# A mixture-of-experts loop re-staged: five turns a page, results queued behind sends, routing in single parts, and a second mixture in four pieces

## The chip, the cores and the metric

One core of one Trainium2 chip runs the whole program. The metric is the device time of one execution in microseconds (us). The engines are TensorE (PE in the profile; PEld is its weight load), VectorE (DVE), ScalarE (ACT), GpSimd (POOL) and SyncE (SP, which only issues DMAs). Each engine works through its own queue in order.

## What is computed

A residual network in float32 on x of shape (4, 1024, 256), four layers one after the other:

```python
x = x + retention(layernorm(x))     # 16 heads, decay mask, gated, group-normalised
x = x + moe(layernorm(x))           # 8 experts, 2 for each token
x = x + rwkv6(layernorm(x))         # a recurrent scan over 1024 steps, 16 heads
x = x + moe(layernorm(x))           # the same router and experts again
```

The mixture is what the change is about:

```python
def moe(t):                                     # t: 4096 tokens x 256
    probs = softmax(t @ Wg.T + bg)              # 8 experts
    topw, topi = top_k(probs, 2)
    topw = topw / sum(topw)
    for e in range(8):                          # combine[:, e] is the token's share, or 0
        gate, up = split(t @ w1[e].T)           # 256 -> 2 x 256
        out += combine[:, e] * ((silu(gate) * up) @ w2[e].T)
    return out
```

## The kernel before

The 4096 tokens are 32 tiles of 128 rows, and eight blocks of four tiles (`NBLK`, `NT`); the residual of block `bk` stays in the on-chip memory as `res[bk]`.

**Pages.** Each mixture computes each token for its two experts only. Tokens are sorted into pages of 128 rows; a page belongs to one expert. 2 x 32 + 7 = 71 pages (`NSL`) always suffice. A token tile is normalised, tagged with its two shares and its number, and written twice into the page buffer `xg_all` in HBM by an indirect DMA that GpSimd issues (`send`, L788). The page loop loads pages in groups of four (`get`, L821), computes, and scatters each page's 128 result rows by another indirect DMA of GpSimd to `y_all` in HBM (`down`, L879). Later `ask` (L916) loads a token tile's two results back and `take` (L927) adds them to the residual on VectorE.

**Pieces.** Tokens come in pieces (`Piece`). The first holds blocks 0 to 3; then follow two pieces of two blocks, here called mid and end. The first piece alone is sure to fill 25 pages (`FULL`); a load of those pages waits for the first piece's sends only, and every load from page 25 on waits for all sends. A piece is routed when its logits are there: `logits` (L549) normalises four tiles on ScalarE, transposes them on TensorE, multiplies with the router, transposes back; `routing` (L597) is a generator whose six parts, called one by one through `route`, pick the two experts (parts one and two, VectorE), rank tokens within an expert by two small matmuls (part three), and work out each token's row (parts four to six). `table` (L759) finds which expert each page belongs to.

**The page loop** (`tiles`, L897) is software-pipelined over three turns. The code of turn j, in the order in which every engine gets it:

```python
if j + 1 < NSL: self.fetch(j + 1)    # transpose page j+1 (PE), copy to m_xt (ACT)
if j < NSL:     self.up(j)           # m_hp (PE), silu m_sg (ACT), product m_a (DVE)
...
if 0 <= j - 1 < NSL: self.turn(j - 1)   # transpose m_a (PE), copy to m_aT (DVE)
if j > 1:            self.down(j - 2)   # m_op (PE), scale to m_y (ACT), scatter (POOL)
for f, *a in extra.get(j, ()): f(*a)    # other work planned for this turn
```

In both mixtures the queues of TensorE, ScalarE, VectorE and GpSimd hold exactly this written order (`manual_schedule`). `extra` holds the rest: routing and sends of the later pieces, `ask` and `take` of the first 16 tiles from turn 41 on, in the first mixture also the end of the retention (`rest`) and the preparation of the scan's first block (`prepare`, L1344), in the second the end of the scan (`finish`, L1383).

**Around it.** The retention runs 32 chunks (loop at L1519); the first piece of the first mixture is sent from chunk 26 on, and the second piece's logits are made in chunks 29 and 31. Then w2a is loaded (L1556) and the page loop starts. During the scan the second mixture's first piece is routed and sent. After the second page loop the last 16 tiles are asked for and taken (L1688 to L1691), and each finished block is stored (`done`, L944).

## Time and profile before

| | |
|---|---|
| Timed runs | 1568.88 us (median of 3, 1567.33 to 1575.58) |
| Profiled execution | 1572.42 us, of which 1570.6 us is the span from first to last instruction |
| Mean granted TensorE clock | 0.918 |
| First page loop, first to last m_sg | 357.7 to 649.1 us |
| Second page loop, first to last m_sg | 1278.4 to 1540.1 us |
| Last scatter issued | 1545.3 us |

The costliest groups in the two page loops, from the page. Columns: line, engine, operation, output <- inputs, count; then busy us in all and mean ns of one; then the idle time of that engine just before such instructions and what ended most of it.

```profile
L888 POOL DMA_INDIRECT y_all<-m_y,m_to x142 | 137.7, 969 | 299.8 <-ACT m_xt L840 169.7
L845 PE MATMUL m_hp<-w1a,m_xt 128*128 x568 | 287.1, 630 | 14.3 <-ACT m_xt L840 11.0
L882 PE MATMUL m_op<-w2a,m_aT 128*128 x568 | 150.8, 389 | 12.0 <-DVE m_aT L877 7.1
L794 POOL DMA_INDIRECT xg_all<-m_row,m_at x128 | 125.1, 977 | 48.7 <-issue 32.6
L838 PE MATMUL m_xtp<-cst,m_xg 128*128 128x128 f32 x284 | 57.9, 288 | 6.1 <-DMA m_xg<-xg_all 6.1
```

A matmul's mean is longer than its share of the time, because matmuls overlap; 142 is two mixtures of 71 pages. A line of slices in the page has 40 digits, one for each fortieth of the span (39.3 us), in tenths.

### The profile page before, as it was taken

How to read it: one execution, taken by the hardware profiler on the slowest of the kernel's cores; microseconds unless marked ns; L12 is line 12 of the kernel's file. 1: busy time of each engine (PE TensorE's matmuls, PEld its weight loads, DVE VectorE, ACT ScalarE, POOL GpSimd, SP SyncE). 2: the span in 40 equal slices, each digit the busy share in tenths (PEclk: the TensorE clock that was granted, in tenths of full speed). 3: DMA queues.
4: the chain of work that ended last, by engine and by line, in shares of the span. 5: the costliest groups of instructions: out<-in, count | busy, mean ns of one | idle time of the engine just before them, and what ended most of it. 6: DMA issues, size and time to landing. Idle time of an engine off the chain costs nothing.

```text
span 1570.6 us, 21231 instructions
## 1 busy us (share of the span) xinstructions
PE 1323.9 (84%) x6700; PEld 680.1 (43%) x6700; DVE 997.4 (64%) x1914; ACT 645.7 (41%) x1646; POOL 892.1 (57%) x854
## 2 busy tenths in 40 slices
PE   5999998958889989998979797889787567899993
PEld 3666665635446544422223232233222124456561
DVE  6666667425433343299978788989998963433544
ACT  2343434333533333445535464545445143433331
POOL 4233323643553225399988888887789935543331
PEclk9999999978789999998979798989898688999997
DMA  8992111131332341267665454534555831332645
GB/s 294 327 320 78 55 55 54 63 118 54 131 112 90 120 125 62 64 144 181 161 143 150 119 135 120 141 101 121 134 161 136 243 112 65 113 99 85 195 125 184
DMA packets 117549, 207.72 MB, mean 132 GB/s; under 512 B 12192, under 2 KB 80000, under 8 KB 117440
## 3 DMA queue, kind: packets, MB, share of 16 engines
q1 hardware_dynamic: 95904, 160.20, 36.3%
q0 software_dynamic: 17184, 39.86, 8.2%
q10 hardware_dynamic: 4352, 6.29, 1.3%
q8 instruction: 57, 0.93, 0.3%
q14 instruction: 52, 0.43, 0.1%
HBM read 139.18 MB, written 67.14 MB: 131 GB/s over the span
## 4 chain that ended last, share of the span: by engine, by line
PE 51%; DVE 16%; POOL 15%; ACT 7%; issue 6%; DMA 3%; another core or an unknown queue 1%; SPq 0%; POOLq 0%; DVEq 0%; ACTq 0%
PE m_hp L845 14%; POOL w_s L1177 7%; PE m_op L882 6%; DVE w_s L1169 4%; PE w_pp L1081 4%; PE a_qkp L311 3%; POOL w_xf L1047 2%; PE a_yp L370 2%; DVE w_vb L1167 2%; POOL w_xf L1050 2%; PE m_xtp L838 2%; PE a_gp L293 2%; PE m_atp L875 2%; PE a_op L245 2%; PE a_sp L350 2%
## 5 line engine op out<-in xcount | busy, mean ns | idle before, releaser
L1177 POOL TENSOR_TENSOR w_s<-w_s,w_rT 128x1024 f32<-128x1024 f32 x128 | 304.5, 2415 | 39.3 <-DVE w_s L1169 29.5
L888 POOL DMA_INDIRECT y_all<-m_y,m_to x142 | 137.7, 969 | 299.8 <-ACT m_xt L840 169.7
L845 PE MATMUL m_hp<-w1a,m_xt 128*128 x568 | 287.1, 630 | 14.3 <-ACT m_xt L840 11.0
L851 DVE TENSOR_TENSOR m_a<-m_hp,m_sg 128x256 f32<-128x256 f32 x142 | 60.1, 423 | 274.4 <-ACT m_sg L849 257.7
L1169 DVE TENSOR_TENSOR_SCAN w_s<-w_wk,w_carry,w_vb 128x512 f32<-128x512 f32 x128 | 160.9, 1276 | 17.0 <-ACT w_carry L1187 4.6
L1167 DVE TENSOR_TENSOR w_vb<-w_vb,w_wk 128x1024 f32<-128x1024 f32 x128 | 153.1, 1196 | 17.1 <-ACT w_wk L1110 15.9
L1169 DVE TENSOR_TENSOR_SCAN w_s<-w_wk,w_vb 128x512 f32<-128x512 f32 x128 | 152.8, 1215 | 14.6 <-PE w_yp L1200 7.4
L882 PE MATMUL m_op<-w2a,m_aT 128*128 x568 | 150.8, 389 | 12.0 <-DVE m_aT L877 7.1
L794 POOL DMA_INDIRECT xg_all<-m_row,m_at x128 | 125.1, 977 | 48.7 <-issue 32.6
L845 PEld LDWEIGHTS m_hp<-w1a,m_xt 128*128 128x128 f32 x568 | 103.8, 203 | 91.4 <-issue 77.6
L1200 PE MATMUL w_yp<-w_s,core_c 128*32 128x512 f32 x512 | 97.0, 672 | 41.7 <-POOL w_s L1177 33.2
L849 ACT ACTIVATE m_sg<-m_hp 128x256 f32<-128x256 f32 x142 | 54.4, 383 | 167.8 <-PE m_hp L845 143.3
L887 ACT ACTIVATE m_y<-m_op,m_share 128x256 f32<-128x256 f32 x142 | 67.2, 473 | 119.1 <-PE m_op L882 90.0
L882 PEld LDWEIGHTS m_op<-w2a,m_aT 128*128 128x128 f32 x568 | 98.8, 194 | 23.8 <-ACT m_y L887 9.4
L323 POOL TENSOR_TENSOR a_t<-a_t,a_t 128x512 f32<-128x512 f32 x32 | 41.0, 1282 | 117.5 <-DVE a_t L322 95.1
L1047 POOL TENSOR_TENSOR w_xf<-w_xf,w_sx 128x512 f32<-128x512 f32 x60 | 78.2, 1303 | 33.2 <-ACT w_xf L1046 32.6
L353 DVE TENSOR_TENSOR a_pt<-a_sp,ret_c 128x2048 f32<-128x2048 f32 x32 | 73.2, 2286 | 17.1 <-PE a_sp L350 17.0
L875 PEld LDWEIGHTS m_atp<-cst,m_a 128*128 128x128 f32 x284 | 40.4, 145 | 89.5 <-issue 70.8
L1050 POOL TENSOR_TENSOR w_xf<-w_xf,w_xT 128x512 f32<-128x512 f32 x64 | 69.7, 1090 | 6.1 <-DVE w_xf L1044 1.4
L840 ACT COPY m_xt<-m_xtp 128x256 f32<-128x256 f32 x142 | 51.9, 365 | 29.4 <-PE m_xtp L838 28.2
L875 PE MATMUL m_atp<-cst,m_a 128*128 128x128 f32 x284 | 55.7, 278 | 9.0 <-DVE m_a L851 5.7
L838 PE MATMUL m_xtp<-cst,m_xg 128*128 128x128 f32 x284 | 57.9, 288 | 6.1 <-DMA m_xg<-xg_all 6.1
(312 smaller groups left out, 2448.5 us busy)
## 6 DMA issues: line engine op xcount, KB each, us to landing
w_vb<-v_all SPq DMA_DIRECT2D x125, 512.0 KB
xg_all<-zero SPq DMA_DIRECT2D x34, 520.0 KB
m_xg<-xg_all SPq DMA_DIRECT2D x34, 520.0 KB
tab<-in_rope SPq DMA_DIRECT2D x32, 512.0 KB
m_back<-y_all SPq DMA_DIRECT2D x48, 256.0 KB
v_all<-w_vT SPq DMA_DIRECT2D x64, 128.0 KB
res<-in_x SPq DMA_DIRECT2D x8, 512.0 KB
w1a<-in_w SPq DMA_DIRECT2D x8, 512.0 KB
```

Source lines behind the costliest of these rows:

```text
L794: nc.gpsimd.indirect_dma_start(out=self.moe.sends[2 * (self.start * NT + i) + n][:, :], out_offset=bass.IndirectOffsetOnAxis(ap=self.at[n] ...
L838: nc.tensor.transpose(tp[:, c, :], self.xg[g][:, i, c * P : (c + 1) * P], ident)
L845: mm(hp, lhsT=self.xt[j][:, c, :], rhs=w1a[:, bass.ds(self.ev[j], 1), c, :].rearrange("p o n -> p (o n)"), start=(c == 0), stop=(c == KC - 1))
L875: nc.tensor.transpose(tp[:, c, :], self.act[j][:, c * P : (c + 1) * P], ident)
L882: mm(op, lhsT=self.aT[j][:, c, :], rhs=w2a[:, bass.ds(self.ev[j], 1), c, :].rearrange("p o n -> p (o n)"), start=(c == 0), stop=(c == KC - 1))
L888: nc.gpsimd.indirect_dma_start(out=self.scatters[j][:, :], out_offset=bass.IndirectOffsetOnAxis(ap=self.to[g][:, i : i + 1], axis=0), in_= ...
L1047: nc.gpsimd.tensor_mul(xf, xf, sx)
L1050: nc.gpsimd.tensor_add(xf, xf, d["now"][:, c, :])
L1167: nc.vector.tensor_mul(vb, vb, wk[:, 1:2, :].to_broadcast([P, 2, BLK]))
L1169: nc.vector.tensor_tensor_scan(s[:, q, 1 : BLK + 1], wk[:, 0, :], vb[:, q, :], 0.0 if j % NB == 0 else st[j - 1]["carry"][:, n, 2 * h + q ...
L1177: nc.gpsimd.tensor_mul(s[:, :, 0:BLK], s[:, :, 0:BLK], d["r"][:, g, :].unsqueeze(1).to_broadcast([P, 2, BLK]),)
L1200: mm(d["yp", g][32 * q : 32 * q + 32, :], lhsT=w["sel"][:, i, :], rhs=d["s", n, q // 2][:, q % 2, 0:BLK], start=False, stop=(i == 3), skip ...
```

## The change

- **Page loop.** Turn j now fetches page j+2, does up of page j, turn of page j-2 and down of page j-4. `m_xt`, `m_a` and `m_aT` get three buffers instead of two, `m_to` four.
- **Scatters.** `down` no longer scatters; it appends its page to a list. After a turn's other work, `tiles` issues scatters from the list as long as a count of indirect DMAs (two for each send, one for each scatter) is below 7/3 a turn, or while more than `LAG` = 8 pages wait. `m_y` gets 12 buffers.
- **Routing.** The six parts of a piece's routing go to four turns, as 1, 2, 1, 2. In the retention the first piece's parts go to chunks 23 and 24, its sends start at chunk 25, and of the second piece's last logits only the normalising stays in chunk 31; the rest is done in turn 0.
- **Start.** The first two page groups are loaded ahead of w2a.
- **Sends.** First mixture: turns 5 to 12 and 14 to 21 (before 4 to 11 and 12 to 19). Second: turns 3 to 10, 11 to 14 and 15 to 18.
- **Pieces.** The second mixture has four: blocks 0 to 3, 4 and 5, 6, 7. `ask` and `take` run in the loop for all pieces but the last, so that 4 tiles instead of 16 are left for the end.
- **Scan.** The statistics of a block are worked out a turn ahead of its normalisation; `prepare` starts two turns later in the loop.

```diff
@@ class Moe
-        def __init__(self, layer):
+        def __init__(self, layer, pieces):
...
-            self.pieces = [Piece(self, 0, HB)]
-            for n in range(HB, NBLK, NB):
-                self.pieces.append(Piece(self, n, NB, self.pieces[-1]))
+            self.pieces, n = [], 0
+            for k in pieces:
+                self.pieces.append(Piece(self, n, k, self.pieces[-1] if n else None))
+                n += k
@@ down
-            y = px.tile([P, C], F32, name="m_y", tag="m_y", bufs=4)
+            y = self.y[j] = px.tile([P, C], F32, name="m_y", tag="m_y", bufs=LAG + 4)
             nc.scalar.activation(y, op, AF.Copy, scale=self.share[g][:, i : i + 1])
+            self.late.append(j)
+
+        def scatter(self):
+
+            j = self.late.pop(0)
+            g, i = self.group[j]
             nc.gpsimd.indirect_dma_start(
                 out=self.scatters[j][:, :],
...
@@ tiles
+            spent = 0
             self.fetch(0)
+            self.fetch(1)
             self.expert(0)
-            for j in range(NSL + 2):
-                if j + 1 < NSL:
-                    self.fetch(j + 1)
+            for j in range(NSL + 4):
+                if j + 2 < NSL:
+                    self.fetch(j + 2)
                 if j < NSL:
                     self.up(j)
                 if j + 1 < NSL:
                     self.expert(j + 1)
-                if 0 <= j - 1 < NSL:
-                    self.turn(j - 1)
-                if j > 1:
-                    self.down(j - 2)
+                if 0 <= j - 2 < NSL:
+                    self.turn(j - 2)
+                if j > 3:
+                    self.down(j - 4)
+                spent = max(spent, 7 * j // 3)
                 for f, *a in extra.get(j, ()):
                     f(*a)
+                    spent += 2 * (f.__name__ == "send")
+                while self.late and (spent < 7 * (j + 1) // 3 or len(self.late) > LAG):
+                    self.scatter()
+                    spent += 1
+            while self.late:
+                self.scatter()
@@ retention's chunks
-        if i in (24, 25):
-            for _ in range(PARTS // 2):
+        if i in (23, 24):
+            for _ in range((2, 4)[i - 23]):
                 m.route()
-            if i == 25:
-                m.table(0)
-        if i >= 26:
-            for t in range(3 * (i - 26), min(3 * (i - 25), HT)):
+        if i == 26:
+            m.table(0)
+        if i >= 25:
+            for t in range(3 * (i - 25), min(3 * (i - 24), HT)):
                 m.send(t)
...
-        if i in (29, 31):
-            mid.logits((i - 29) // 2)
-            mid.biased((i - 29) // 2)
-    for _ in range(2):
-        mid.route()
+        if i == 29:
+            mid.logits(0)
+            mid.biased(0)
+        if i == 31:
+            mid.tokens(1)
@@ first mixture
-    load(w2a, w2)
     px = pool("px", "right")
     px2 = banks("px2")
+    for g in range(2):
+        moes[0].get(g)
+    load(w2a, w2)
...
+    def back_to(moe, pieces):
+
+        for p in pieces:
+            lo, hi = p.start * NT, p.start * NT + p.nt
+            start = 2 * hi + E - 1 + 4
+            for i in range(lo, hi):
+                add(start + i - lo, moe.ask, i)
+                add(start + 2 + i - lo, moe.take, i)
...
+    add(0, mid.turned)
+    add(0, mid.product)
+    add(0, mid.flipped)
+    add(0, mid.biased, 1)
...
-    for n, j in enumerate((1, 1, 2, 3)):
+    for j in (1, 2, 2, 3, 4, 4):
         add(j, mid.route)
...
+    for j in (10, 11, 11, 12, 13, 13):
+        add(j, end.route)
+    pieces_sent(moe, (5, 14))
@@ second mixture
-    for j, n in ((1, 1), (2, 2), (3, 3), (4, 4), (5, 5), (5, 6), (5, 7)):
+    for j, n in ((0, 1), (1, 2), (3, 3), (4, 4), (5, 5), (6, 6), (6, 7)):
         add(j, finish, n)
...
+    for j in (3, 4, 4, 5, 6, 6):
+        add(j, late.route)
...
+    for j in (9, 10, 10, 11, 12, 12):
+        add(j, end.route)
+    pieces_sent(moe, (3, 11, 15))
+    back_to(moe, moe.pieces[:3])
     moe.tiles(extra)
...
-    for i in range(HT, TT):
+    for i in range(TT - NT, TT):
         moe.ask(i, pe)
-    for i in range(HT, TT):
+    for i in range(TT - NT, TT):
         moe.take(i)
```

## The prediction, made before the result was known

> **What bounds the kernel now.** I read the page's slices first, then stage windows, then the waits of TensorE and the queue of GpSimd inside the two stages that the change touches. From the page, and from the stage windows (columns: window, length, then busy us and instruction count of PE, PEld, DVE, ACT, POOL, then granted clock, DMA share, GB/s):
>
> ```profile
> PE   5999998958889989998979797889787567899993
> PEclk9999999978789999998979798989898688999997
> ...
> 357.70:473.30 115.60, 97.21 (x361) 57.29 (x362) 54.67 (x216) 46.72 (x120) 60.90 (x67) 0.86 0.32 102
> 473.30:539.80 66.50, 66.50 (x266) 41.04 (x265) 24.18 (x85) 24.61 (x67) 22.29 (x28) 1.00 0.29 93
> 539.80:649.10 109.30, 99.76 (x349) 54.34 (x348) 44.90 (x147) 38.70 (x94) 45.93 (x50) 0.97 0.29 91
> 1278.40:1397.30 118.90, 94.67 (x360) 54.49 (x361) 49.72 (x205) 50.87 (x126) 55.89 (x59) 0.90 0.27 86
> 1397.30:1463.80 66.50, 66.50 (x267) 41.04 (x266) 22.40 (x81) 24.63 (x67) 19.20 (x20) 1.00 0.30 95
> 1545.30:1570.60 25.30, 0.00 (x0) 0.00 (x0) 12.51 (x32) 0.00 (x0) 0.96 (x1) 0.54 0.77 257
> ```
>
> The mixture's loop has two regimes. In the second and fifth windows 22 pages take 66.50 us with PE never idle: **3.02 us a page, and TensorE is the bound**. No reordering goes below that. In the other three windows PE is idle 18.4, 9.5 and 24.2 us (length minus busy) and part of its busy time is at half clock: a clock of 0.86 means 2 x 0.14 x 115.6 = 32 us at half rate. Work at full clock in the first window is 23 pages x 3.02 = 69.5 plus about 16.5 for router logits and last projections (their PE rows, cleaned of half rate) = 86, so 11 us of the 97.2 are the clock. The same sum gives 4 in the third window and 10 in the fourth. So 52 us of idle and 25 of clock, 77 in all, is the most that these two loops can give back. The last window is a tail with PE at nothing.
>
> What ends PE's idle time in the first window, and what GpSimd does there (its queue in order of time; L888 scatters a result, L794 sends a token tile):
>
> ```profile
> PE m_hp L845 <- ACT m_xt L840: 4.7, 1, 4.7
> PE m_xtp L237 <- ACT m_row L792: 3.3, 2, 1.6
> PE m_atp L875 <- DVE m_a L851: 2.6, 2, 1.7
> PE m_op L882 <- DVE m_aT L877: 2.6, 3, 1.1
> PE m_lpT L569 <- ACT m_lT L565: 2.3, 2, 1.2
> ...
> 447.98 0.96 POOL L794 DMA_INDIRECT xg_all<-m_row,m_at  x1 [0.30 <-issue]
> 449.24 0.96 POOL L794 DMA_INDIRECT xg_all<-m_row,m_at  x1 [0.30 <-issue]
> 453.43 0.96 POOL L888 DMA_INDIRECT y_all<-m_y,m_to  x1 [3.23 <-ACT m_y L887]
> 454.69 0.96 POOL L794 DMA_INDIRECT xg_all<-m_row,m_at  x1 [0.30 <-issue]
> 455.96 0.96 POOL L794 DMA_INDIRECT xg_all<-m_row,m_at  x1 [0.30 <-issue]
> ```
>
> The waits are short and spread over all of a page's links; each is an engine answering PE inside the same turn. GpSimd goes scatter, send, send, and when the scatter waits for its page the sends behind it wait too. Three issues are 3 x 1.26 = 3.8 us, more than a page's 3.02.
>
> **The change, part by part.**
>
> *Pages over five turns.* Up, turn and down now lie two turns apart and the fetch two ahead, so the links have a page more of slack, about 3 us. In the first window the 4.7 (ACT stuck behind the retention's normalising), 2.6, 2.6, and 1.4 + 1.2 that the waits list below those lines go: 12.5. In the third window all but 2 of 9.5 goes: its largest, 4.15 us, is ACT waiting for the scan's statistics, which also start a turn earlier. In the fourth window I take out 3.8 (the output projection behind GpSimd's w_sq, now a turn later), 3.4 (a wait with no named cause), 2.1, 1.8, 2.8 on DVE's m_a, and 1.7 + 0.8: 16.4. PE work added: none. Down-phase drain: PE ends with five downs instead of three, which cost 1.5 to 1.7 us apart at the end of the trace, but has one turn and two downs less queued before; I count +1 us.
>
> *What stays.* Router logits (4 of them) keep their transposes waiting for ACT in the same turn: 5.6 and 4.2 us. The 3.3 us of w_rp behind DVE's w_rstd stays, since root and spread_out remain in one turn.
>
> *Routing one part a turn.* Twice a turn holds two parts, and one pair is part two (nine DVE operations of 0.22 us) and part three (the rank matmuls that need them). PE then waits about 2 us in its own order; four times (two pieces in each mixture), 4 us a mixture. In before this pair was split for the last piece and showed 1.7 once. Bounds: 0 if DVE runs ahead, 3 each if it lags.
>
> *Results behind sends.* The counter allows 7/3 indirect issues a turn, 2.95 us of GpSimd against 3.02 of PE. By its arithmetic the backlog reaches eight and is gone by turn 28. Sends stop being held up. This is how the waits above can go at all, so it has no term of its own; m_y grows to 12 buffers, so ACT isn't held.
>
> *A new wait at page 25.* Pages from 25 on need every send landed. In the first mixture the last send moves from turn 19 to turn 21, while page 25 is fetched at turn 23 instead of 24. In the trace the last send issues at 464.02 and the load behind it on SP's queue at 466.65, 1.7 us after the issue ended. After turn 21's last matmul: 0.8 for ACT's row, 2.5 for two sends, 1.7 landing, 3.7 for the load (the chain's m_xg row) = 8.7, of which turn 22 covers 3.0. **PE stalls 5.7 us**, with ACT and DVE behind it. Ends: 2 (GpSimd ahead, load at the 2.2 us of the first page), 10 (backlog of three more issues). In the second mixture the last send is at turn 18, so nothing.
>
> *The clock.* The Trainium skill, "TensorE: Matmul & The Clock Gate", section "The HAM clock gate", has the clock halve after an idle window of about 3.4 us and return after a busy one. By that rule the first window, with one wait over 3.4, would lose 3.4/2 = 1.7 us; the row says 32 us at half rate, 11 lost. Here waits of 1 to 2 us close together halve it too, so I go by the row and let the clock loss shrink with the idle time: 11 to 7, 4 to 1, 10 to 6, which is 11 us. By the rule it would be near 3.
>
> *Start.* Page loads move ahead of the w2a load on SP's queue, and the last logits of the second piece move into turn 0. Before, PE ended retention at 335.3, SP was let go at 340.8 and the first m_sg came at 357.7. Now: load at 340.8, landed 343.1, transposes, second page 345.6 (a load of 3.7), up at half clock 3.5, m_sg near 349.5. That is 8.2, less 2.7 of PE work and 1.2 of wait moved into the loop: 4.3. Routing a chunk earlier in retention: +-2, taken as 1 gained.
>
> *Four pieces and the tail.* Twelve of the last 16 output tiles are taken inside the loop, on DVE that is idle there (37 of 76 us). The tail now:
>
> ```profile
> 1545.33 0.96 POOL L888 DMA_INDIRECT y_all<-m_y,m_to  x1 [0.78 <-ACT m_y L887]
> 1548.02 11.12 SPq L922 DMA_DIRECT2D m_back<-y_all  x16
> 1554.69 10.50 DVE L931 TENSOR_TENSOR res<-m_back,res 128x256 f32<-128x256 f32 x26 [0.75 <-DMA m_back<-y_all]
> 1559.19 6.40 SPq L947 DMA_DIRECT2D out<-res  x4
> ```
>
> Last scatter to first add takes 5.5 us and last add to end 5.4; between lie 32 adds in 14.3. Eight adds take 8 x 0.42 = 3.4, so the tail falls by 10.9, less the +1 of the drain: 10. The fourth piece costs one more routing (PE 0.5; DVE has room) and six more asks, of which two wait for all scatters: PE idled 0.7 us for such a pair at 1467, covered now.
>
> **Sum.** First loop: 12.5 - 4 - 5.7 + 4 (clock) = 6.8; third window 7.5 + 3 = 10.5; second mixture 16.4 - 4 - 0.5 + 4 = 15.9; start 4.3, retention 1, tail 10: **48.5 us**. The profiled execution took 1572.42 (span 1570.6 and 1.8 around it), so 1523.9; the median of the timed runs is 3.5 lower, which gives **1521**.
>
> **Rivals.**
> *Only the ends land* (0.14): engines run in order, so the waits reappear one or two turns later and the loops keep their 77 us; start, retention and tail give 15.3, and a third of the loops' 33 gives 11: 1543. For it: the logits and w_rp waits lie inside one turn.
> *All slack is turned into pages* (0.15): idle falls to the logits' 10 us and the clock stays near 1. The loops give 77 - 10 - 5 = 62 and the ends 15: 1492. For it: the flat 3.02 for 22 pages.
> *Page loads held behind asks* (0.08): SP runs in order, and each ask waits for a take on DVE, so the load of a group of four pages comes late for PE, which now fetches two ahead. There are 11 such groups (4 + 7). In before a scatter-ask round cost 2.4 + 2.7 us; at 4.4 us a group the gain is gone, and at 6 the time is 1521 + 66 = 1587, slower. Against it: before has the same order ask, take, load in the same turns, and PE shows no wait for m_xg there.
> *The gain is paid back at page 25 and in routing* (0.04): the upper ends, 10 + 12, with the clock unchanged and half of the removed waits back: about 1566.
>
> **How the numbers follow.** The forecast has 0.59. Its own range, from the bounds of page 25, routing and clock, is 1500 to 1540. The range given reaches into the first two rivals: 1490 to 1552. A change under 0.5% (8 us) could not be told from none: same 0.04, slower 0.08, faster 0.88.
>
> **What would show it.** Right: flat 3.02 us pages start near page 12 instead of 23; scatters lag sends between turns 5 and 21; a PE wait on DMA m_xg near page 25 of the first mixture alone; four m_back loads and eight adds after the last scatter. Wrong: PE waits for m_xg at pages 45 to 69 (the loads behind asks), or the clock row still at 0.86 with the named waits gone (the clock isn't tied to them).

## The result, and the profile after

| | before | after |
|---|---|---|
| Timed runs, median of 8 | 1569.55 us (1563.89 to 1575.58) | 1556.10 us (1551.92 to 1559.71) |
| Ratio after / before | | 0.9915, 95% interval 0.9894 to 0.9936 |
| Profiled execution, span | 1572.42, 1570.6 | 1556.23, 1554.3 |
| Mean granted TensorE clock | 0.918 | 0.925 |

The change is faster by 13.4 us (0.85%). The forecast was 48 us faster, 1521, and its range ended at 1552: the sign was right, and three quarters of the gain did not come. Where it went is read by stage. The table takes the two profiled executions, cut at the first `m_sg` of each loop, at page 26, and at the last `m_y`:

| Stage (us) | before | after | difference | the prediction's terms |
|---|---|---|---|---|
| Start to first page | 357.7 | 349.6 | -8.1 | -9.2 (5.3, and 3.9 of work moved into the next stage) |
| First loop, pages 0 to 26 (its send stage) | 124.7 | 129.4 | **+4.7** | -6.8 + 3.9 = -2.9 |
| First loop, page 26 to last m_y | 171.2 | 161.5 | -9.7 | -10.5 |
| Scan, to the second loop's first page | 624.8 | 628.6 | +3.8 | 0 |
| Second loop, pages 0 to 26 (its send stage) | 128.0 | 128.7 | **+0.7** | -15.9 |
| Second loop, page 26 to last m_y | 138.2 | 140.4 | +2.2 | +1 |
| Last m_y to last scatter | 0.7 | 2.8 | +2.1 | 0 |
| Tail | 25.3 | 13.1 | -12.2 | -10.9 |

So the start, the third window and the tail did what the sum said. The two send stages, which were to give 18.8 net, got 5.4 us longer.

From the page after, the slices of TensorE and of its clock:

```profile
PE   5999998877879999997878888888787567979995
PEclk9999999878989999999989898999898779989998
```

The sagging stretch of the first loop (digits 9 to 13) is still there. The stage windows after (window, length, then busy us and count of PE, PEld, DVE, ACT, POOL, then clock, DMA share, GB/s):

```profile
349.60:479.10 129.50, 100.23 (x414) 60.32 (x413) 58.98 (x243) 53.90 (x134) 61.27 (x68) 0.89 0.31 99
...
539.80:640.90 101.10, 98.51 (x358) 54.85 (x357) 44.29 (x144) 39.41 (x95) 48.90 (x53) 1.00 0.32 102
1269.20:1397.90 128.70, 103.61 (x390) 58.74 (x391) 62.23 (x266) 55.64 (x135) 56.79 (x60) 0.89 0.26 84
...
1541.10:1554.30 13.20, 0.00 (x0) 0.00 (x0) 3.25 (x8) 0.00 (x0) 0.96 (x1) 0.50 0.41 140
```

The second line is the success: PE idles 2.6 us where it idled 9.5, at a clock of 1.00. The first and third are the failure, the two send stages: 29.3 and 25.1 us of idle, more than the 18.4 and 24.2 of the same pages before, at a clock that stays below 0.9. What ended PE's idle time in the first of them, from the waits (us in all, times, longest):

```profile
PE m_rank L657 <- DVE m_dif L640: 10.3, 2, 8.6
PE m_xtp L844 <- DMA m_xg<-xg_all: 6.8, 1, 6.8
PE m_op L888 <- ACT m_y L893: 6.6, 2, 4.3
```

The old waits (4.7 for ACT's m_xt, 2.6 for m_a, 2.6 for m_aT) are gone, as predicted. In their place stand three others: routing's rank matmul, the wait at page 25, and a wait for m_y that the prediction doesn't have. In the second send stage, the largest miss, the longest are:

```profile
PE m_op L888 <- ACT m_y L893: 4.4, 2, 3.9
PE m_op L888 <- issue: 4.1, 1, 4.1
PE m_hp L851 <- DVE m_a L857: 3.8, 2, 2.8
PE m_rank L657 <- DVE m_dif L640: 3.7, 2, 2.2
```

Here only the waits for GpSimd's w_sq (3.8 before, 0.8 now) and for m_aT (1.8 before) went as predicted. Those for m_y, for "issue" and for DVE's m_a, taken out at 2.1, 3.4 + 0.8 and 2.8, stand at 4.4, 4.1 and 4.8.

The tail, from the timeline (start, length, engine, what, idle before and its releaser):

```profile
1533.55 0.97 POOL L900 DMA_INDIRECT y_all<-m_y,m_to  x1 [5.89 <-DVE res L954]
...
1541.14 0.96 POOL L900 DMA_INDIRECT y_all<-m_y,m_to  x1 [0.30 <-issue]
1543.70 2.17 SPq L945 DMA_DIRECT2D m_back<-y_all  x4
1548.41 1.68 DVE L954 TENSOR_TENSOR res<-m_back,res 128x256 f32<-128x256 f32 x4 [0.29 <-DMA m_back<-y_all]
```

Four loads and eight adds instead of 16 and 32. But the first line shows GpSimd idle for 5.89 us until an add of `take`: a piece's first two asks read all of y_all, and the scatters behind them wait for them. Seven scatters then run in a row, and the last one comes 2.8 us after the last m_y instead of 0.7.

### The profile page after: what moved, and what is told of

The parts are those of the page before. It is cut to its first block, busy times and chain, and to the rows that moved or that the text cites. A ratio compares the mean times of both kernels' runs of the same rounds, so it can differ in the third digit from the quotient of the medians.

```text
span 1554.3 us, 20957 instructions
## 1 busy us (share of the span) xinstructions
PE 1313.1 (84%) x6704; PEld 675.9 (43%) x6704; DVE 1004.7 (65%) x1963; ACT 648.7 (42%) x1649; POOL 891.2 (57%) x854
## 4 chain that ended last, share of the span: by engine, by line
PE 57%; DVE 14%; POOL 11%; ACT 8%; issue 5%; DMA 2%; another core or an unknown queue 2%; POOLq 0%; SPq 0%; DVEq 0%; ACTq 0%
PE m_hp L851 15%; PE m_op L888 7%; PE w_pp L1108 5%; POOL w_s L1204 5%; DVE w_s L1196 4%; PE a_qkp L315 3%; PE a_yp L374 2%; DVE w_vb L1194 2%; PE m_xtp L844 2%; PE w_dp L1056 2%; PE a_op L249 2%; PE a_sp L354 2%; PE a_gp L297 2%; PE m_atp L881 2%; POOL w_xf L1074 2%
## 5 line engine op out<-in xcount | busy, mean ns | idle before, releaser
L851 PE MATMUL m_hp<-w1a,m_xt 128*128 x568 | 283.2, 623 | 3.8 <-DVE m_a L857 3.8
L900 POOL DMA_INDIRECT y_all<-m_y,m_to x142 | 137.5, 969 | 211.8 <-ACT m_xt L846 145.4
L1194 DVE TENSOR_TENSOR w_vb<-w_vb,w_wk 128x1024 f32<-128x1024 f32 x128 | 153.3, 1198 | 18.8 <-ACT w_wk L1137 17.6
L1227 PE MATMUL w_yp<-w_s,core_c 128*32 128x512 f32 x512 | 92.3, 645 | 47.7 <-POOL w_s L1204 38.0
L844 PE MATMUL m_xtp<-cst,m_xg 128*128 128x128 f32 x284 | 58.3, 289 | 13.5 <-DMA m_xg<-xg_all 13.3
L1227 PEld LDWEIGHTS w_yp<-w_s,core_c 128*32 128x32 f32 x512 | 14.2, 113 | 112.4 <-POOL w_s L1204 59.4
## 6 DMA issues: line engine op xcount, KB each, us to landing
v_all<-w_vT SPq DMA_DIRECT2D x64, 128.0 KB
```

Of the source, the lines that this page charges most:

```text
L844: nc.tensor.transpose(tp[:, c, :], self.xg[g][:, i, c * P : (c + 1) * P], ident)
L851: mm(hp, lhsT=self.xt[j][:, c, :], rhs=w1a[:, bass.ds(self.ev[j], 1), c, :].rearrange("p o n -> p (o n)"), start=(c == 0), stop=(c == KC - 1))
L900: nc.gpsimd.indirect_dma_start(out=self.scatters[j][:, :], out_offset=bass.IndirectOffsetOnAxis(ap=self.to[g][:, i : i + 1], axis=0), in_= ...
L1194: nc.vector.tensor_mul(vb, vb, wk[:, 1:2, :].to_broadcast([P, 2, BLK]))
L1227: mm(d["yp", g][32 * q : 32 * q + 32, :], lhsT=w["sel"][:, i, :], rhs=d["s", n, q // 2][:, q % 2, 0:BLK], start=False, stop=(i == 3), skip ...
```

## The experiments

The runs fell on several chips. On some, before takes 1538 to 1541 us, on others, like the one of the prediction, 1567 to 1570. So each ratio is to before on the same chip. Each profile is of one execution, which can lie some us from the median of its kernel. Two theories: **A**, TensorE is held up by GpSimd's long unbroken runs of indirect DMAs; **B**, the gain was eaten by waits in the order of the queues, which the change makes itself.

### Results not held back

```diff
-                while self.late and (spent < 7 * (j + 1) // 3 or len(self.late) > LAG):
+                while self.late:
```

> The change with one edit: a page's scatter is issued in the turn of its down, behind that turn's sends, with no count and no backlog. Theory A (GpSimd streaks: TensorE is held for several us while GpSimd issues eight or more indirect DMAs without a gap, and the backlog of scatters makes such streaks at pages 19 to 24): the streaks of 12 to 16 issues vanish, streaks of three per turn come back; within 6 us of the change's 1556. Theory B (letting results wait is what the gain in the loops rests on, as the prediction had it): sends are held up again, 3.8 us a turn for 16 turns in each mixture, 12 to 25 us slower, about 1575.

Measured: 1539.38 us, ratio 0.9999 (0.9986 to 1.0012). Without the waiting list the change gains nothing. With the list, the ratio on such chips is 0.9911 (the change, below), and a kernel whose order in the send stages is the change's took 1529.2 us on this very chip (the run "Results held, then released at once"). So the list is worth some 10 to 13 us. The two send stages take 128.4 and 116.1 us here, against 124.1 and 110.1 in that kernel: 10.3 us. PE's wait at page 25, without the list and with it, in the first and then in the second loop:

```profile
PE m_xtp L844 <- DMA m_xg<-xg_all: 14.1, 1, 14.1
PE m_xtp L844 <- DMA m_xg<-xg_all: 8.4, 1, 8.4
...
PE m_xtp L844 <- DMA m_xg<-xg_all: 4.3, 1, 4.3
PE m_xtp L844 <- DMA m_xg<-xg_all: 0.3, 1, 0.3
```

That is 9.7 of the 10.3 us; PE's other waits agree within 1.0 us. So on this chip the list does not free the page's links. It lets the last send, and with it the load of page 25, go earlier.

### Three turns instead of five

```diff
-            self.fetch(1)
...
-                if j + 2 < NSL:
-                    self.fetch(j + 2)
+                if j + 1 < NSL:
+                    self.fetch(j + 1)
...
-                if 0 <= j - 2 < NSL:
-                    self.turn(j - 2)
-                if j > 3:
-                    self.down(j - 4)
+                if 0 <= j - 1 < NSL:
+                    self.turn(j - 1)
+                if 1 < j < NSL + 2:
+                    self.down(j - 2)
```

> The change with the page loop back at three turns: fetch of page j+1, turn of j-1, down of j-2; everything else stays. If the slack of five turns removed the 29 us of waits that the prediction took out: 20 to 35 us slower, 1576 to 1590. If the waits were only the visible side of something else that binds in the send stage (theory A): under 8 us slower, and page 25 of the first mixture waits some 3 us less, since it is fetched a turn later.

Measured: 1528.73 us, ratio 0.9930 (0.9906 to 0.9954), which can't be told from the change. By stage, against the same kernel of this chip as above, the five turns shorten the send stages by 1.7 and 2.5 us (125.8 and 112.6 here), 4.2 in all. They lose more elsewhere: the second loop's first page comes 6.5 us earlier with three turns (625.0 against 631.5 after the first loop's end), and its drain is 2.9 us shorter (137.5 against 140.4). Of the 6.5, 2.0 lie at the loop's start, where two pages are transposed ahead of the first up and not three; the other 4.5 arise within the scan, and no run shows why. (This profiled execution, at 1523.70, is 5 us below the median of its kernel.)

### Routing's parts two and three apart

```diff
-    for j in (1, 2, 2, 3, 4, 4):
+    for j in (1, 2, 3, 3, 4, 4):
         add(j, mid.route)
...
-    for j in (10, 11, 11, 12, 13, 13):
+    for j in (10, 11, 12, 12, 13, 13):
         add(j, end.route)
```

and in the second mixture (3, 4, 5, 5, 6, 6) and (9, 10, 11, 11, 12, 12).

> The change with parts two and three of routing in different turns: 1, 2, 3, 3, 4, 4 in place of 1, 2, 2, 3, 4, 4, and likewise for the other three pieces routed in a loop. Theory C (the pair is what eats the gain): the waits of the rank matmul, 8.6 + 1.7 us in the first and 2.3 + 1.5 in the second mixture, go, and the time with them: 10 to 18 us faster, 1538 to 1546. Theory A: most of it comes back as other waits in the same stage; 0 to 5 us faster.

Measured: 1518.41 us, ratio 0.9867 (0.9839 to 0.9895); the kernel of the next run, on the same chip, took 1526.46 to 1529.42 and this one 1515.86 to 1522.12. The pairs cost some 7 us by the ratios (0.9911 for the change) and 11 by the medians of these two kernels. Why, the timeline of the change shows, around its largest wait:

```profile
358.51 1.52 ACT L437 ACTIVATE a_yn<-a_yT,a_shift,a_scale 128x512 f32<-128x512 f32 x2 [3.36 <-DVE a_shift L432]
...
363.31 0.42 DVE L857 TENSOR_TENSOR m_a<-m_hp,m_sg 128x256 f32<-128x256 f32 x1 [1.34 <-ACT m_sg L855]
363.99 0.21 DVE L621 TENSOR_REDUCE m_top<-m_rest 128x8 f32<-128x64 f32 x1
365.63 0.66 PE L657 MATMUL m_rank<-m_both,cst 128*128 128x64 f32 x2 [8.58 <-DVE m_dif L640]
```

PE stands at the rank matmul from 357.06. Part two of the routing lies in DVE's queue behind this turn's m_a. That waits for m_sg, and m_sg stands in ACT's queue behind the retention's normalising (a_yn, four instructions), which itself waits for DVE and GpSimd. PE stands still for a chain through three engines, not for DVE's nine operations. It is the place of the largest wait of before as well: the 4.7 us for m_xt stood behind the same four a_yn. With the parts in separate turns, the waits of the same stage are:

```profile
PE m_xtp L844 <- DMA m_xg<-xg_all: 9.1, 1, 9.1
...
PE m_rank L657 <- DVE m_dif L640: 1.3, 1, 1.3
```

10.3 became 1.3. Part of it is waited for later: the wait at page 25 grew to 9.1.

### Results held, then released at once

```diff
-                while self.late and (spent < 7 * (j + 1) // 3 or len(self.late) > LAG):
+                while self.late and not (28 <= j < 42 and j != 34) and (j == 34 or j == 42 or spent < 7 * (j + 1) // 3 or len(self.late) > LAG):
```

> The change with scatters held back in the quiet part of both loops, where no sends run: none in turns 28 to 33 and 35 to 41, all waiting ones at once in turns 34 and 42, so that GpSimd issues seven or eight indirect DMAs without a gap, four times in all. The work is the same. Theory A: the pages that run during a burst take longer than 3.02 us, by 2 to 8 us for each burst, with no wait named in the trace: 8 to 30 us slower. If streaks do nothing to TensorE: all pages stay at 3.02 us and the time stays within 3 us of 1556.

Measured: 1529.2 us, ratio 0.9924 (0.9899 to 0.9949), no change; every page of these turns stays at 3.02 us. But the edit made no bursts. GpSimd around turn 34, which starts at 489.9:

```profile
488.74 0.96 POOL L900 DMA_INDIRECT y_all<-m_y,m_to  x1 [2.06 <-ACT m_xt L846]
491.77 0.96 POOL L900 DMA_INDIRECT y_all<-m_y,m_to  x1 [2.06 <-ACT m_xt L846]
```

One scatter a page, as in before. Apart from the copies of turn 29 (`inputs`), GpSimd's queue holds only scatters in these turns, so holding them back in the code leaves their order as it was, and each goes as soon as its result is there. The run says nothing on theory A; it serves as a second run of the change's order. What speaks against A on this chip are its send stages, where GpSimd issues up to 37 indirect DMAs in a row and no page is held up by it (below).

### Before and after on one chip

> The kernel before, unchanged, for a profile of it on the same chip as the runs beside it. Theory one (the send stages lost their gain to waits that the change itself makes, the same on every chip): pages 0 to 26 of the second mixture take about as long here as with the change, 110 us each. Theory two (on the first chip TensorE was held up there by something that the change does not make): before needs 10 us or more above the change's 110 here, as it should by the prediction's 15.9.

> The changed kernel, unchanged, beside the other runs. Ratio to before 0.9915 if the gain is the same on every chip; 0.985 or less if the first chip held up the changed kernel alone. Send stages (pages 0 to 26) of about 124 and 110 us, as in the run with the held scatters, whose code is the same there.

Measured: before 1541.02 us (17 runs), the change 1528.16, ratio 0.9911 (0.9887 to 0.9935), the same as on the first chip. The send stages, from the windows of before and then of the change:

```profile
351.10:463.10 112.00, 97.96 (x397) 59.61 (x397) 58.01 (x229) 50.31 (x129) 63.64 (x70) 0.94 0.35 113
1257.00:1374.30 117.30, 99.15 (x396) 57.89 (x397) 52.84 (x218) 54.30 (x135) 59.03 (x62) 0.93 0.29 95
```

```profile
342.90:466.90 124.00, 100.90 (x413) 60.92 (x412) 58.98 (x243) 53.99 (x133) 61.36 (x68) 0.88 0.31 101
1259.00:1368.60 109.60, 94.92 (x391) 54.74 (x392) 61.49 (x266) 55.97 (x136) 54.71 (x58) 0.95 0.30 97
```

Before needs 12.7 and 10.7 us less here than on the first chip. So a part of the idle and half-clock time that the prediction meant to win back was no slack of the page's links. PE's waits of before's first send stage here say which:

```profile
PE m_hp L845 <- ACT m_xt L840: 4.1, 1, 4.1
PE m_xtp L838 <- DMA m_xg<-xg_all: 3.1, 1, 3.1
PE m_atp L875 <- DVE m_a L851: 1.8, 1, 1.8
```

Of the 28.9 us of waits that the term "Pages over five turns" takes out, before has 14.2 here: 4.1 and 1.8 in the first send stage; 3.8 (w_sq), 2.8 (m_a) and 1.7 (m_rank) in the second. Those for m_aT, for m_y and for "issue" are not there, and from page 14 to 22 its pages follow at a flat 3.02 us in both loops. At page 25 before waits too here, 3.1 and 2.7 us. On this chip the first send stage gets 12.0 us worse with the change and the second 7.7 better, between the nothing of theory one and the 10 or more of theory two.

### The last piece two turns earlier

```diff
-    add(5, end.block, 0)
-    add(7, end.block, 1)
+    add(3, end.block, 0)
+    add(5, end.block, 1)
...
-    for n, j in ((0, 7), (1, 9)):
+    for n, j in ((0, 5), (1, 7)):
...
-    for j in (10, 11, 11, 12, 13, 13):
+    for j in (8, 9, 9, 10, 11, 11):
         add(j, end.route)
-    pieces_sent(moe, (5, 14))
+    pieces_sent(moe, (5, 12))
```

> The last piece of the first mixture is routed and sent two turns earlier (sends in turns 12 to 19 instead of 14 to 21), page 25 is still fetched in turn 23. If the wait at page 25 is the prediction's new wait (last send, landing, load), it falls by two turns, from 7 to 8 us to about 2, and the kernel is 5 to 6 us faster than the change (0.35%). If TensorE only waits there for a backlog of GpSimd that is as long in any case (eight scatters and all sends), the wait stays above 5 us and the time is the change's.

Measured: 1520.95 us (1519.07 to 1525.79), ratio 0.9866 (0.9841 to 0.9891), 7.2 us faster than the change beside it (1526.16 to 1530.41). The waits of its first send stage:

```profile
PE m_rank L657 <- DVE m_dif L640: 11.4, 2, 8.6
PE m_xtp L844 <- DMA m_xg<-xg_all: 3.7, 1, 3.7
```

The wait at page 25 fell from 8.3 to 3.7; the stage went from 124.0 to 117.1, more than the wait, and its clock from 0.88 to 0.93. It is the prediction's new wait (before has 3.1 there), and it costs clock as well.

### Sixteen tiles left for the end again

```diff
-    back_to(moe, moe.pieces[:3])
+    back_to(moe, moe.pieces[:1])
...
-    for i in range(TT - NT, TT):
+    for i in range(HT, TT):
         moe.ask(i, pe)
-    for i in range(TT - NT, TT):
+    for i in range(HT, TT):
         moe.take(i)
```

> Four pieces stay, but only the first piece's tiles are asked for and taken inside the second loop; 16 tiles are left for the end, as before. The prediction's sum gives a tail longer by 10.9 us; the trace of the change says that its asks in the loop also held the last scatters by 2 to 4 us, which this edit gives back. So 7 to 9 us slower than the change (0.5 to 0.6%) if both are right, 11 us if the held scatters cost nothing, and no difference if the end is bound elsewhere.

Measured: 1536.24 us, ratio 0.9966 (0.9951 to 0.9982), 8.1 us slower than the change beside it. From its timeline:

```profile
1510.18 0.96 POOL L900 DMA_INDIRECT y_all<-m_y,m_to  x1 [0.74 <-ACT m_y L893]
```

The last scatter follows its m_y at once (0.7 us), and the tail is 24.2 instead of 13.3: 10.9 longer, less the 2.4 by which the change's asks hold the scatters.

### Both mends together, three turns, and w2a first

The first kernel has the split pairs and the earlier last piece (`end.route` in turns 8, 9, 10, 10, 11, 11); the second has three turns besides, as above; the third is the change with one edit:

```diff
-    for g in range(2):
-        moes[0].get(g)
     load(w2a, w2)
+    for g in range(2):
+        moes[0].get(g)
```

> The change with both mends at once: routing's parts two and three in turns of their own, and the first mixture's last piece two turns earlier. Each gave about 7 us alone (ratios 0.9867 and 0.9866 against 0.9911). If the rank wait and the wait at page 25 are two separate losses, their sum is 14 us and the ratio 0.982 to 0.983. If one only uncovers the other (what PE gains early it waits for at page 25), the ratio stays at 0.986 to 0.987.

> The same two mends, with the page over three turns as before (fetch one ahead, turn one behind, down two behind); results still wait behind sends. If the five turns bring what the prediction took (slack for every link of a page), it is 5 us or more slower than the run with five turns. If the slack was never the bound, it is equal or up to 5 us faster, since the drain is shorter (137.5 against 140.4 us after page 26 of the second loop) and the second loop's first up waits for one page and not for two.

> The change with w2a loaded ahead of the first two page groups again. If the earlier first page of the first loop (8 us in both traces) is due to this order, PE waits some 7 us for its first page instead of 3, and the kernel is 4 to 8 us slower than the change (ratio 0.994 to 0.996). If the gain there comes from the routing and the logits that moved, it is equal to the change (0.991).

Measured, where before takes 1567.31: both mends 1548.51, ratio 0.9879 (0.9852 to 0.9906); three turns 1550.16, 0.9891 (0.9869 to 0.9912); w2a first 1561.47, 0.9962 (0.9946 to 0.9979).

The order of the loads is worth 0.47% against the change's 0.9915, which is from another chip of this kind: some 7 us, with 3 to 12 inside the two intervals. The first page comes 4.2 us later than with both mends (354.7 against 350.5). The waits at the start, w2a first and then the kernel with both mends, which has the change's order:

```profile
PE m_xtp L844 <- DMA m_xg<-xg_all: 10.3, 2, 9.7
```

```profile
PE m_xtp L844 <- DMA m_xg<-xg_all: 4.8, 2, 3.3
```

Three turns are again equal to five. But both mends gave 0.0036, some 5.6 us, where 14 were expected (the change's 0.9915 again from the other chip). The waits of the first send stage with both mends say why:

```profile
PE m_op L888 <- issue: 12.5, 3, 6.6
PE m_op L888 <- ACT m_y L893: 2.4, 2, 2.1
PE m_rank L657 <- DVE m_dif L640: 2.1, 1, 2.1
```

The two mended waits are down to 2.1 and nothing; 15 us of waits at m_op stand in their place, which on the other chips are not there. The 6.6 us of "m_op <- ACT m_y" of the change are of the same kind. One of these pauses, from the timeline of the change:

```profile
1357.24 1.88 PE L851 MATMUL m_hp<-w1a,m_xt 128*128 x4
1359.18 1.03 PE L888 MATMUL m_op<-w2a,m_aT 128*128 x4
1367.15 2.07 PE L888 MATMUL m_op<-w2a,m_aT 128*128 x4 [3.93 <-ACT m_y L893]
...
1365.15 0.38 ACT L855 ACTIVATE m_sg<-m_hp 128x256 f32<-128x256 f32 x1 [5.32 <-remote]
...
1363.46 0.96 POOL L900 DMA_INDIRECT y_all<-m_y,m_to  x1 [0.31 <-issue]
```

By PE's modelled ends the four m_hp matmuls were done at 1359.1, but ACT, idle for 5.32 us, took them only at 1365.15; the signal of PE's semaphore comes 6 us late. PE itself had gone on: by the records of semaphores in the trace, the next five signals, for work that takes PE some 3 us, came within 1.6 us of that one. PE's wait for m_y at 1367.15 is the echo. GpSimd had issued eleven indirect DMAs without a break by then.

As late counts here an instruction of ACT or DVE in the page loops that, its engine idle, starts about 2 us or more after the modelled end of the matmul that it reads. The eight profiles from chips of this kind, before's among them, have 5 to 13 each, 2 to 11 us late, all in the two send stages and each during a run of 6 to 22 issues of GpSimd. Such runs fill 27 to 38% of these stages. The twelve profiles of the other kind have none, with runs of up to 41 issues.

### GpSimd paced

Both mends once more, and with these edits (then also with three turns):

```diff
-LAG = 8
+LAG = 14
...
-                to = self.to[g] = px.tile([P, GRP], I32, name="m_to", tag="m_to", bufs=4)
+                to = self.to[g] = px.tile([P, GRP], I32, name="m_to", tag="m_to", bufs=6)
...
-                spent = max(spent, 7 * j // 3)
+                spent = max(spent, 2 * j)
...
-                while self.late and (spent < 7 * (j + 1) // 3 or len(self.late) > LAG):
+                while self.late and (spent < 2 * (j + 1) or len(self.late) > LAG):
```

> The change with both mends (routing's parts two and three apart, last piece two turns earlier), once more, beside the paced kernel. On the chip where before takes about 1540 us the ratio should be near 0.982 (two separate losses of 7 us), on the one where it takes about 1568 us near 0.988 as measured there, because TensorE then pauses in the send stages.

> The two mends, and GpSimd's indirect DMAs paced at two a turn instead of 7/3, with room for 14 results in waiting: two issues take 2.5 of a turn's 3.0 us, so GpSimd pauses each turn and its unbroken runs of 9 to 40 issues end. If long unbroken runs of GpSimd's issues are what TensorE pauses at (theory one), the pauses of 2 to 8 us go on a chip that shows them, the send stages fall by some 10 us each, and the kernel is 10 to 20 us faster than the one beside it. If the pauses come from the send stage's load as such (theory two: as many DMAs, as many rows), they stay and the time is equal within 3 us. On a chip without pauses it is equal in either case.

> The paced kernel with the page over three turns. If the five turns are worth nothing once the two mends and the pacing are in, it is equal to the paced kernel with five turns or up to 5 us faster (shorter drain, the second loop's first up waits for one page). If slack matters once nothing else holds TensorE, it is 5 us or more slower.

Measured, where before takes 1567.87: both mends 1552.92 (0.9886, 0.9858 to 0.9915), paced 1546.89 (0.9868, 0.9846 to 0.9890), three turns paced 1549.15 (0.9883, 0.9858 to 0.9909). The intervals overlap, so this is no verdict. Nor was the supposed cause taken away: when 14 results wait, the list is forced, and at the end of the stages came runs of 18 to 22 issues with delays of 2 to 11 us.

### More scatters where there are no sends

Two pairs of runs put more indirect DMAs into the flat stage of the first mixture, pages 45 or 46 to 65, on top of both mends. In the first pair each result is scattered to the same rows three times or twice (`for _ in range(3 if ... else 1)` around the scatter). In the second the additional scatters go to two tables that nothing reads:

```diff
+            for n in range((2 if j % 3 else 0) if self.layer == 0 and 45 <= j < 66 else 0):
+                nc.gpsimd.indirect_dma_start(
+                    out=self.twins[n].pop()[:, :],
...
```

and `(j % 2)` as the count in the sparse one.

> The change with both mends; in the first mixture each result of pages 46 to 65 is scattered three times to the same rows, where no sends are, so that GpSimd needs 3.8 us for a page of 3.0 and issues some 60 indirect DMAs without a break in a stage that runs at a flat 3.02 us a page. If unbroken runs of issues are what TensorE pauses at, pauses of 2 to 8 us appear there on a chip whose send stages show them (some six, 20 us or more in all). If the pauses belong to the sends, the stage stays at 3.02 us a page.

> The same with each of these results scattered twice, 2.5 us of GpSimd for a page of 3.0, so with a pause in every turn. If only unbroken runs matter, the stage stays at 3.02 us a page; if the mere number of indirect DMAs matters, pauses come here too, about two thirds of the other's.

> The change with both mends; in the first mixture two of three pages from 45 to 65 are scattered twice more, into two tables that nothing reads, so that GpSimd issues 7 indirect DMAs in three turns (2.95 us of 3.02 a page) in a stage without sends that runs at a flat 3.02 us a page. If dense issuing is what TensorE pauses at, pauses of 2 to 8 us appear there on a chip whose send stages show them; if they belong to the sends, or on a chip without pauses, the stage stays flat.

> The same with every second of these pages scattered once more, 4.5 issues in three turns (1.9 us of 3.02 a page), with a gap in every turn. If dense, unbroken issuing is the cause, the stage stays flat here; if each indirect DMA has its share in the pauses, some come here too.

Measured, one execution each: 1585.22 and 1535.26 where before took 1539.96; 1512.59 and 1510.23 where before took 1538.01. The first pair tells nothing. A scatter to the same rows waits for the landing of the one ahead of it, as in the run with two:

```profile
569.12 0.96 POOL L901 DMA_INDIRECT y_all<-m_y,m_to  x1 [3.89 <-DMA y_all<-m_y,m_to]
```

The issues did not follow each other, and with three of them PE waited 33.8 us for an m_y. The second pair issues as meant, in runs of up to ten, but both fell on a chip without delays, and there dense issuing delayed no page: PE idles 1.0 us from 520 to 600 us. (The loop's last m_y came 4.5 us later than in the sparse run, in the drain.) It does show both mends on such a chip: 0.982 with the sparse scatters, the 0.982 to 0.983 expected of two separate losses. What the delays come from on the other chips stays open.

## Why the prediction was right in sign and wrong in size

**Right.** The third window (-9.7 against -10.5). The page-25 wait: 6.8 us against 5.7, in the predicted place and in the first mixture alone; the last send was issued at 455.75, and PE went on at 462.21. The tail: -12.2 against -10.9. Undoing it costs 8.1, less than the term of 10, for the sum had nothing for scatters held by asks. The start: -8.1 against -9.2; the 7 us of the load order, with 3 to 12 inside the intervals, agree with the term of 4.3. The rival "page loads held behind asks" found nothing: PE waits for no m_xg from page 26 on. One sign of being right did not come: flat pages "near page 12 instead of 23". On the prediction's chip they start at page 26; on the other kind they run from page 13 to 21, where before's are flat from 14 on as well.

**Wrong: "Pages over five turns".** This is the step that failed. It took 12.5 and 16.4 us out of the send stages because the waits that the trace names sit on a page's links. The three-turn run measures the term: the five turns give 4.2 us in the two send stages, not 28.9, and take 9.4 back in the scan with the second loop's start and in the drain, of which the sum had 1. With both mends in, three turns and five were equal twice more. Two things were wrong in it. First, 14.7 of the 28.9 us are waits that before does not have where no signal of TensorE comes late; in the prediction's trace they are, but for 1.4 us, those for m_aT, for m_y and for "issue", in the stages where such delays are, and I counted them as slack of the links. Second, the engines run in order, and a wait removed let PE run on to the next thing that it needs in the same turn: the 4.7 us for m_xt went, and 8.6 at the rank matmul came, behind the same a_yn.

**Wrong: "Results behind sends … has no term of its own".** Without it the change is worth nothing where before takes 1540, and it gives 10.3 us in the send stages there, 9.7 of them at page 25. The sum has no gain there, only the new wait.

**Mis-sized: "Routing one part a turn".** The sum had 2 us for each of four pairs and an upper end of 3, from nine DVE operations. The four waits measured 8.6, 1.7, 2.2 and 1.5: three as priced, and one four times as long. The text asked what PE waits for, and not what stands ahead of it in DVE's queue. Mended, this gave 7 to 11 us on one chip.

**Mis-sized: the clock.** I took 11 us back from the half-rate time, 4 and 4 of it in the send stages. The clock there (pages 0 to 26) went from 0.87 to 0.89 and from 0.91 to 0.89, for it follows the waits, and these were replaced. Windows of the change, laid on the steps of the granted clock:

```profile
434.30:441.10 6.80, 3.83 (x16) 2.15 (x14) 0.24 (x1) 0.81 (x3) 4.39 (x5) 1.00 0.31 109
441.20:448.00 6.80, 5.52 (x10) 3.07 (x11) 2.94 (x10) 2.92 (x9) 3.70 (x4) 0.50 0.18 61
448.00:458.20 10.20, 7.39 (x31) 4.52 (x29) 3.14 (x13) 4.25 (x12) 5.88 (x7) 1.00 0.22 78
```

PE pauses at 438.1 for 4.3 us; at 441.2 the clock falls to 0.50 and comes back 6.8 us later. PE works for 5.5 us of these, so the pause costs some 2.8 us more. The pauses of 8.6 and 6.8 us cost 1.9 and 1.4 by the same reading. The rule of the Trainium skill ("TensorE: Matmul & The Clock Gate", section "The HAM clock gate"), an idle window of about 3.4 us, fits these three, but not the row as a whole. From before, after 24 us at full clock in which PE's only long wait was one of 1.6 us, at 393.3:

```profile
396.90:403.60 6.70, 5.54 (x23) 2.62 (x24) 1.74 (x6) 1.16 (x3) 4.78 (x8) 0.50 0.54 188
```

So the prediction was right that short waits halve the clock too. What failed is that the idle time, with which the loss was to shrink, grew from 18.4 to 29.3 us in the first send stage and from 24.2 to 25.1 in the second. The text had named the sign: the clock row still low with the named waits gone.

**Not in the sum: the scan** got 3.8 us longer here and 7.9 on the other chip. The three-turn runs are 2.5 to 6.5 us shorter there than their five-turn neighbours; what makes the rest of it is not shown. **And the delays** of TensorE's signals on chips like that of the prediction. They stay with the change, and the mends give some 8 of 14 us less where they are; that the delays take them is argued from the waits at m_op, not shown by an experiment. One reading was loose as well: the 37 of 76 us are DVE's busy time, its idle time is 39.

The rival that came nearest, in number and in mechanism, is "the gain is paid back at page 25 and in routing", at about 1566 with a chance of 0.04: the clock unchanged, routing's waits at 14.0 us where its upper end had 12, and page 25 at 6.8. "Only the ends land", at 1543, had the waits that reappear a turn later.

The best versions tried are the change with both mends, 0.988 to 0.989 of before on chips like the first, and the same paced, 0.987, which can't be told from it; the change has 0.9915. On the other chips both mends have 0.982 to 0.983 in single executions, with additional scatters.

## What to carry to other kernels

A wait that the profile names on a link is not yet slack that a deeper pipeline gives back: ask what PE needs next in the same turn, and what stands ahead of it in the queue of the engine that delivers it. A wait that the same kernel does not show on another chip can't be counted as such slack. Price a pair of dependent steps by the whole queue of the supplying engine, here 8.6 us and not 2 in the one turn where another layer's work stood in that queue. Look in the trace whether a test made what it was to make: code that holds an instruction back changes nothing when its queue holds nothing else. A transfer that has to come after all sends is priced from the last send, and moving that send two turns earlier is worth more than the wait, since the clock comes back with it.

## What the runs showed of the hardware that was not expected

- The same two kernels differ by 1.8% from chip to chip (before 1540 and 1568 us) at the same ratio, 0.991. The difference lies mostly in stages with many indirect DMAs: of the 32 us between before's two profiled spans, 23 are in its send stages.
- On the slower chips PE's signals came 2 to 11 us late, 5 to 13 times in a profile and always during a run of 6 to 22 of GpSimd's indirect DMAs; on the faster ones runs of up to 41 delayed nothing. Whether the runs are the cause was not shown.
- In the send stages a stretch of half clock lasts a multiple of 3.41 us (most often 3.4, 6.8 or 10.2), so a pause of 4.3 us was followed by 6.8 at half rate.
